# Up products of paired 256-token tiles as seven fp32 block products in the shared expert

## The chip, the cores and the metric

The kernel runs on one NeuronCore of a Trainium2 chip. The engines are TensorE (PE, matrix products into PSUM), VectorE (DVE), ScalarE (ACT), GpSimd (POOL) and SyncE (SP, which here only issues DMA). Each engine works through its own instruction list in order and waits on semaphores that other engines or DMA transfers raise. The metric is the device time of one execution in microseconds. Before the change it is 723.63 us (median of three runs, 723.37 to 724.58).

## What is computed

All data are fp32. Sixteen sequences of 128 tokens with 256 features pass through a cross-attention layer (16 heads of 64) with a residual, then through a mixture of experts with a residual:

```
x = x + attention(context, layernorm(x), cond)          # per sequence
h = layernorm(x)                                        # 2048 tokens x 256
scores = h @ router                                     # 2048 x 8
expert = argmax(scores); gate = sigmoid(max score)      # top 1
shared = (silu(h @ ws1) * (h @ ws3)) @ ws2              # ws1, ws3: 256 x 704; ws2: 704 x 256
routed = silu(gate*h @ w1[e]) * (gate*h @ w3[e]) @ w2[e]
out = x + shared + routed
```

The change concerns `shared` alone, and the order in which parts of it run.

## The kernel before

**Stages.** The attention runs over pairs of sequences (`g` = 0 to 7) in steps `u` of eight heads. In most steps (`seven_step`) the key and value projections are made as seven block products instead of eight; `plain_step` is used for `u` = 0, 1 and 31. `seven_step` is built of `product` (TensorE), `hold` (a ScalarE copy out of PSUM) and `join` (a VectorE add). A step makes logits on TensorE, negated row maxima on VectorE (L672), exponentials on ScalarE (L679), a division by the row sums on GpSimd (L692), a transposition in 32x32 blocks on VectorE (L701) and through DRAM (L705, L713), and then the weighted sums on TensorE (L725) for the step before.

After that, normalised tokens are transposed into `hT` (feature by token), the router's scores decide the expert of each token (`route`, a chain of many small VectorE operations), and eight expert windows are worked through: `up` (L1607 to L1620), `out_rows` (L1640), which adds the residual and the shared part gathered from `s_rows`, and an indirect scatter to `out` (L1645).

**The shared expert.** Its tokens form eight tiles of `TB` = 256. Of the 704 hidden columns, `FC` = 5 blocks of 128 are full; the last 64 columns of `ws1` and of `ws3` share one block. For a tile, `hidden(t, mid, f)` makes for a full block two products with 256-long sums, that is four fp32 products of 128 x 128 by 128 x 256 (L164), silu on ScalarE (L179) and a multiply on VectorE (L180); the narrow block takes two products. `down` makes 12 products (L194), adds the residual (L201) and stores to `s_rows`. A tile so has 22 + 12 products.

The generator `shared_expert` yields after each block, and `shared_unit()` advances it by one piece wherever TensorE would have to wait: in the last two attention steps, between the last projections, and in the routing chain (one piece for each step of `route`). The down products of a tile are made after the hidden blocks of the next one. Tile 7 is kept to the end (`held`): its hidden block 0 before the last window's down products, the rest after them. It reads `out` back (L236), after every scatter, adds its rows (L254) and stores them (L255).

**Order and memory.** The order on each engine is written out by hand: instructions run in the order in which the Python code calls them. PSUM has three pools: `ps_s` (two tiles of two banks), `ps_m` (three of one bank, tag `mm`, shared by `hidden`, `down` and most other users) and `ps_o` (one). A tile's wait is derived from who last read or wrote it.

Of the kernel before, what the change touches and what calls it, by code (L numbers as in the profile page):

```python
# [9 lines left out]
F32 = mybir.dt.float32  # L10
I32 = mybir.dt.int32
AF = mybir.ActivationFunctionType
ALU = mybir.AluOpType
# [4 lines left out]
P = 128  # L18
# [9 lines left out]
def resampler_attn__then__top1_moe_kernel(  # L28
# [160 lines left out]
    def down(t, mid, xr):  # L189
        rows = slice(t * TB, (t + 1) * TB)  # L190
        py = ps_m.tile([P, 2, D], F32, tag="mm", name=f"ys_{t}")
        for i in range(2):
            for f in range(FC + 1):
                nc.tensor.matmul(  # L194
                    py[:, i, :],
                    lhsT=mid[:, f, ts(i, P)],
                    rhs=shared["wd"][:, f, :],
                    start=(f == 0),
                    stop=(f == FC),
                )  # L200
        nc.vector.tensor_tensor(xr, py, xr, ALU.add)  # L201
        nc.gpsimd.dma_start(out=s_rows[rows, :].rearrange("(b p) d -> p b d", p=P), in_=xr)

    def shared_expert():


        pend = None
        for t in range(NT // TB - 1):
            rows = slice(t * TB, (t + 1) * TB)
            xr = mwork.tile([P, 2, D], F32, tag="xr", name=f"xr_{t}", bufs=3)  # L210
            nc.gpsimd.dma_start(out=xr, in_=x_rows[rows, :].rearrange("(b p) d -> p b d", p=P))
            mid = mwork.tile([P, FC + 1, TB], F32, tag="mid", name=f"mid_{t}")
            nc.gpsimd.memset(mid[0 : P - FR, FC, :], 0.0)
            for f in range(FC + 1):
                hidden(t, mid, f)
                yield
            if pend is not None:
                down(*pend)
                yield
            pend = (t, mid, xr)  # L220
        yield "last"
        down(*pend)
        yield
# [3 lines left out]
    def held(mid):  # L227

        t = NT // TB - 1
        xr = mwork.tile([P, 2, D], F32, tag="xr", name=f"xr_{t}", bufs=3)  # L230
        nc.gpsimd.memset(mid[0 : P - FR, FC, :], 0.0)
        for f in range(FC + 1):
            hidden(t, mid, f)
            yield
        for i in range(2):
            load = nc.sync.dma_start(out=xr[:, i, :], in_=out[B - 2 + i])  # L236
            for s in scattered:
                tc.add_manual_dep(
                    load.ins,
                    s.ins.name,  # L240
                    mybir.DependencyInfo(mybir.DependencyClass.Sync, mybir.DependencyReason.DATA),
                    reason="rows of any token may come from any tile",
                )
        for i in range(2):
            py = ps_m.tile([P, D], F32, tag="mm", name=f"ys_{t}_{i}")
            for f in range(FC + 1):
                nc.tensor.matmul(
                    py,
                    lhsT=mid[:, f, ts(i, P)],
                    rhs=shared["wd"][:, f, :],  # L250
                    start=(f == 0),
                    stop=(f == FC),
                )
            nc.vector.tensor_tensor(xr[:, i, :], py, xr[:, i, :], ALU.add)  # L254
            nc.sync.dma_start(out=out[B - 2 + i], in_=xr[:, i, :])  # L255

    def shared_unit():
        return next(stream, None)


    with ExitStack() as at:
# [565 lines left out]
        def norms(gt, gh):  # L827
# [27 lines left out]
            def h_stats():  # L855
                rows = slice(2 * gh * S, (2 * gh + 2) * S)
                xr = xres[gh]
                nc.sync.dma_start(
                    out=x_rows[rows, :].rearrange("(b p) d -> p b d", p=P), in_=xr
                )  # L860
                mv = st["hmv"] = small.tile([P, 2, 2], F32, tag="hmv", name=f"hmv_{gh}")
                for i in range(2):
                    s6 = small.tile([P, 6], F32, tag="hst", name=f"hst_{gh}_{i}")
                    nc.vector.bn_stats(s6, xr[:, i, :])
                    nc.vector.bn_aggr(mv[:, i, :], s6)
# [105 lines left out]
        def plain_step(u, units, side=(), behind=()):  # L971
# [15 lines left out]
            nm = maxima(u, 1, ps[1])  # L987
            unit()
            normalise(u, 0)
            exponents(u, 1, ps[1], nm)  # L990
# [111 lines left out]
        for g in range(NG):  # L1102
# [89 lines left out]
            else:  # L1192
                seven_step(
                    u + 2, Seven("v", g, 1), (), {}, (h_on("h_stats", "h_variances"), roots, (), ()),
# [6 lines left out]
        keep_heads(2 * B - 2)  # L1201
        finish(B - 2)
        for j in range(3):
            shared_unit()
# [3 lines left out]
        shared_unit()  # L1208
# [9 lines left out]
        shared_unit()  # L1218
# [7 lines left out]
    mscratch = scratch.enter_context(tc.tile_pool(name="mscratch", bufs=1))  # L1226

# [4 lines left out]
    w2s = [wexp.tile([P, NF, D], F32, name=f"w2_{k}") for k in range(5)]  # L1232

# [77 lines left out]
    def route():  # L1311
# [57 lines left out]
        pc = ps_m.tile([P, 2, B * E], F32, tag="mm", name="counts")  # L1369
# [172 lines left out]
    def transpose_pair(pair):  # L1542

        px = ps_m.tile([P, DC, 2, P], F32, tag="mm", name=f"px_{pair[0]}")
# [4 lines left out]
        if pair[0] == 0:  # L1549
            nc.vector.tensor_copy(  # L1550
                inputs_t[0][:, :, 0 : 2 * P], px.rearrange("p c i q -> p c (i q)")
# [131 lines left out]
    for w in range(E):  # L1683
        for f in range(NF):
            up(w13s[w % 3], inputs_t[w % NREST], WINDOWS[w], mids[w % 5], f, f"w{w}")
            if f == 0:
# [10 lines left out]
                else:  # L1697
                    shared_unit()
# [9 lines left out]
    def ending():  # L1708
        rest = held(mids[E % 5][:, :, 0:TB])
# [137 lines left out]
```

## Time and profile before

| | us |
|---|---|
| median of three runs | 723.63 |
| profiled execution | 724.18 |
| its span | 722.5 |
| TensorE busy | 708.2 |
| VectorE busy | 415.3 |
| ScalarE busy | 295.0 |
| GpSimd busy | 287.5 |

The span is the profiled execution from its first to its last instruction. Mean granted TensorE clock is 0.995 of full speed. In the timeline, the shared expert begins at 440.24 us; the last attention product of line 725 begins at 473.26, the first expert window at 569.56, and the last down products of tile 7 at 713.02. How a profile row reads: the line of the kernel, engine, operation, the tile written and those read, shape and count; then busy time, mean duration of one in nanoseconds, and the engine's idle time just before, with what ended most of it. In a timeline row come the start, the length, and in brackets the idle time before it. In a row of stretches come, for each engine, busy time and number of instructions, then the granted clock, the DMA share and GB/s.

### The profile page before, as it was taken

The numbers are of one execution on the slowest core, as the hardware profiler recorded it, in microseconds if no ns is written. First come the engines' busy times: TensorE is split into PE (matmuls) and PEld (weight loads), VectorE is DVE, ScalarE is ACT, GpSimd is POOL, SyncE is SP. The second block draws the span as 40 slices with busy tenths as digits, with TensorE's granted clock in tenths as the row PEclk, the third lists the DMA queues.
The fourth block names the chain that finished last, engine by engine and source line by source line (L and its number), as shares of the span: only waits on it lengthen the run. The fifth ranks groups of instructions, "written<-read, shape, count | busy, mean of one in ns | idle before, by whom it ended". The sixth has DMA issues, their size and how long they took to land.

```text
span 722.5 us, 11941 instructions
## 1 busy us (share of the span) xinstructions
PE 708.2 (98%) x4228; PEld 594.8 (82%) x4228; DVE 415.3 (57%) x941; ACT 295.0 (41%) x855; POOL 287.5 (40%) x449
## 2 busy tenths in 40 slices
PE   9999999999999999999999999899899999999997
PEld 6778888888888888888888887688798878878886
DVE  6568678777777777777766766325623333323321
ACT  3555475475475366466466456412111111101111
POOL 4358346346346345435433622311032234434220
PEclk9999999999999999999999999999999999999999
DMA  8266755864864865765764765341393136666601
GB/s 277 73 218 198 219 172 183 242 191 163 252 191 158 253 193 168 235 196 181 206 194 156 255 186 179 104 116 34 129 364 107 44 88 167 198 195 181 188 29 46
DMA packets 140470, 125.20 MB, mean 173 GB/s; under 512 B 61615, under 2 KB 124594, under 8 KB 140404
## 3 DMA queue, kind: packets, MB, share of 16 engines
q1 hardware_dynamic: 135892, 111.46, 49.8%
q0 software_dynamic: 4224, 12.65, 5.5%
q8 instruction: 35, 0.57, 0.3%
q14 instruction: 31, 0.25, 0.1%
q10 hardware_dynamic: 288, 0.26, 0.1%
HBM read 75.59 MB, written 48.92 MB: 172 GB/s over the span
## 4 chain that ended last, share of the span: by engine, by line
PE 92%; DVE 3%; ACT 3%; DMA 2%; issue 1%; ACTq 0%
PE u_w L1607 10%; PE O L725 8%; PE p L164 8%; PE pw L744 8%; PE S L660 8%; PE pq L487 8%; PE yr L1640 6%; PE ys L194 5%; PE skX L606 5%; PE svX L606 5%; PE svZ L606 3%; PE svY L606 3%; PE skZ L606 3%; PE skY L606 3%; ACT pe L679 1%; PE ur_w L1607 1%
## 5 line engine op out<-in xcount | busy, mean ns | idle before, releaser
L692 POOL TENSOR_SCALAR pe<-pe,rs 128x256 f32<-128x256 f32 x256 | 130.4, 526 | 227.3 <-DVE rs L689 227.3
L679 ACT ACTIVATE pe<-S,nmx 128x256 f32<-128x256 f32 x256 | 119.0, 483 | 54.8 <-DVE nmx L672 54.8
L672 DVE TENSOR_REDUCE nmx<-S 128x4 f32<-128x1024 f32 x64 | 75.4, 1219 | 30.9 <-PE S L660 30.9
L701 DVE STREAM_TRANSPOSE px<-pe 128x512 f32<-128x512 f32 x128 | 82.2, 682 | 0.1
L164 PE MATMUL p<-hT,ws 128*128 128x256 f32 x320 | 73.9, 387 | 3.4 <-DVE mid L180 3.3
L1607 PE MATMUL u_w<-xT,w 128*128 128x256 f32 (+2 forms) x320 | 77.1, 396 | 0.0
L164 PEld LDWEIGHTS p<-hT,ws 128*128 128x128 f32 x320 | 61.3, 194 | 13.1 <-DVE mid L180 3.7
L1607 PEld LDWEIGHTS u_w<-xT,w 128*128 128x128 f32 x320 | 60.7, 190 | 13.7 <-issue 0.4
L744 PE MATMUL pw<-wo,oT 128*128 128x256 f32 x256 | 66.3, 385 | 0.0
L487 PE MATMUL pq<-kvT,early 128*128 128x256 f32 x256 | 65.8, 385 | 0.0
L725 PEld LDWEIGHTS O<-pT,v 128*64 128x64 f32 x1024 | 55.2, 137 | 12.3 <-issue 5.6
L725 PE MATMUL O<-pT,v 128*64 128x128 f32 x1024 | 63.2, 276 | 1.4 <-DMA pT<-p_blocks 1.4
L660 PE MATMUL S<-kT,qT 64*128 64x256 f32 x512 | 63.9, 389 | 0.0
L1615 ACT ACTIVATE rsl_w<-u_w 128x256 f32<-128x256 f32 (+2 forms) x40 | 16.0, 400 | 110.6 <-PE u_w L1607 89.2
L487 PEld LDWEIGHTS pq<-kvT,early 128*128 128x128 f32 x256 | 47.5, 190 | 11.0 <-issue 5.1
L736 ACT COPY oT<-O 128x512 f32<-128x512 f32 x32 | 18.7, 586 | 92.2 <-PE O L725 92.2
L744 PEld LDWEIGHTS pw<-wo,oT 128*128 128x128 f32 x256 | 47.4, 190 | 10.6 <-issue 4.8
L660 PEld LDWEIGHTS S<-kT,qT 64*128 64x128 f32 x512 | 46.8, 186 | 10.5 <-issue 6.2
L179 ACT ACTIVATE sl<-p 128x256 f32<-128x256 f32 x40 | 15.2, 383 | 96.9 <-PE p L164 96.9
L679 ACT ACTIVATION_READ_ACCUMULATOR pe<-S,nmx 128x1 f32 x256 | 54.5, 213 | 0.0
L1616 DVE TENSOR_TENSOR mid_w<-u_w,rsl_w 128x256 f32<-128x256 f32 (+2 forms) x40 | 17.8, 445 | 60.3 <-ACT rsl_w L1615 56.1
L1640 PE MATMUL yr<-w,mid_w 128*128 128x256 f32 (+1 forms) x252 | 48.0, 379 | 0.0
(269 smaller groups left out, 1151.1 us busy)
## 6 DMA issues: line engine op xcount, KB each, us to landing
p_blocks<-px SPq DMA_DIRECT2D x64, 512.0 KB
pT<-p_blocks SPq DMA_DIRECT2D x64, 512.0 KB
w<-in_w_dram SPq DMA_DIRECT2D x16, 640.0 KB
w<-in_w_dram SPq DMA_DIRECT2D x8, 704.0 KB
t_blocks<-tx SPq DMA_DIRECT2D x12, 256.0 KB
kvT<-t_blocks SPq DMA_DIRECT2D x12, 256.0 KB
h_rows<-h SPq DMA_DIRECT2D x8, 256.0 KB
xres<-in_x_dram SPq DMA_DIRECT2D x7, 256.0 KB
```

Of the source, the lines that this page charges most:

```text
L164: nc.tensor.matmul(ps, lhsT=shared["w13"][:, c, ds(col, P)], rhs=hT[:, c, ts(t, TB)], start=(c == 0), stop=(c == DC - 1),)
L487: nc.tensor.matmul(pqs[g, j][:, jj], lhsT=wq[:, c, ts(2 * j + jj, P)], rhs=kvTs[g][:, c, :, 1, :], start=(c == 0), stop=(c == DC - 1),)
L606: nc.tensor.matmul(o[:, a, :], lhsT=left, rhs=right, start=(first and a == 0), stop=(a == 1), skip_group_check=True,)
L660: nc.tensor.matmul(pl[:, r, j, :], lhsT=qTs[g, h][rows, k, i, :], rhs=kTs[g, h][rows, i, k, :], start=True, stop=True,)
L672: nc.vector.tensor_reduce(nmx, pl, AX.X, ALU.max, negate=True)
L679: nc.scalar.activation(pes[u][:, h, :], pl[:, r, j, :], AF.Exp, bias=nmx[:, r, j : j + 1], accum_out=sums[u][:, h : h + 1],)
L692: nc.gpsimd.tensor_scalar(w, w, rs[:, i : i + 1], 1.0, ALU.mult, ALU.mult)
L701: nc.vector.transpose(px[:, :, t].rearrange("p j h q -> p h j q"), pes[u][:, ts(n, 4), ts(t, S)].rearrange("p h (j k) -> p h j k", k=BL),)
L725: nc.tensor.matmul(o[r * HD : (r + 1) * HD, j, :], lhsT=vs[g, h][:, i, t, ts(2 * j + r, HD)], rhs=pTs[u][:, j // 2, :, t, 2 * (j % 2) + r, :],
L744: nc.tensor.matmul(pws[b], lhsT=outT[u][:, k % HC, :], rhs=wo[:, k, :], start=(k == 0), stop=(k == NP - 1))
L1607: nc.tensor.matmul(ps[:, k, 0:n], lhsT=w13[:, c, ds(col, P)], rhs=xT[:, c, 0:n], start=(c == 0), stop=(c == DC - 1),)
L1640: nc.tensor.matmul(py[rows, :], lhsT=mid[:, f, :], rhs=wd[:, f, :], start=(f == 0), stop=(f == NF - 1))
```

## The change

1. **Tiles 0 and 1** are made as before. Their down products are now given out in two halves.
2. **Tiles 2 to 7** are taken in three pairs (`pair`, k = 1, 3, 2 in this order). The two sums over 256 features for two matrices (`ws1`, `ws3`) and two tiles are a 2 x 2 by 2 x 2 block product. It is made with seven products a block instead of eight, from sums and differences of weight blocks (`pair_weights`) and of token blocks (`pair_tokens`), both on GpSimd. `place` gives the order of the products in TensorE's list. The partial results meet in PSUM: two X tiles used in turn for even and odd blocks, and one tile whose halves are Y and Z. These three take all of `ps_m` while the pairs run. Three results of a block are copied out by ScalarE, and four adds or multiplies on VectorE and one multiply on GpSimd make the hidden values. The narrow block keeps two products a tile (`left`).
3. **Pair 3** (tiles 6 and 7, the last 512 tokens) writes its hidden values into a buffer `held`; its four half down products and their adds to `out` come at the end, the first before the last window's down products, the second right after them. The loads and stores of `out` alternate between SyncE's and ScalarE's queues.
4. **In `plain_step`** for `u` > 1, the second four heads' exponentials are issued before the shared-expert piece instead of after it. In the last `seven_step`, the Newton steps of the layer norm move behind the join of Y and the hold of X (from the second to the third group of `sides`).
5. The number of pieces given out between the last attention projections changes, `x` of the pair g = 6 goes to `s_rows` instead of `x_rows` (its shared part is added at the end), and three other users of `ps_m` (`counts`, the transposes of gathered rows, the down products) use `ps_s`.

The products by number, and where each is placed (7f + offset):

```
n  offset  writes  operands (weights x tokens)        after it
1    0     X       w1[0]      x a0                     ACT copies X to hs0
5    2     Z       s1         x tt0                    ACT copies Z to high
2    3     Y       w1[1]      x a1                     DVE hs0 = Y + hs0; ACT silu
6    4     X +=    s2         x tt1                    ACT copies X to hs1
3    6     Z +=    s4         x b1                     DVE hs1 = Z + hs1; ACT silu
7    8     X +=    (w1[0]-w3[0]) x tt2                 DVE high = X + high; POOL high *= hs1
4   12     X +=    w3[1]      x tt3                    DVE low = X * hs0
```

The core of the diff:

```diff
+    def pair_tokens(k):
+        ...
+        op = nc.gpsimd.tensor_tensor
+        op(tt[:, 0], blk(0, 1), blk(0, 0), ALU.subtract)
+        op(tt[:, 1], blk(1, 1), tt[:, 0], ALU.subtract)
+        op(tt[:, 2], blk(1, 1), blk(0, 1), ALU.subtract)
+        op(tt[:, 3], blk(1, 0), tt[:, 1], ALU.subtract)
+    def pair_weights(f):
+        ...
+        op(s1, up_block(1, 0, f), up_block(1, 1, f), ALU.add)
+        op(s2, s1, up_block(0, 0, f), ALU.subtract)
+        op(up_block(1, 0, f), up_block(0, 0, f), up_block(1, 0, f), ALU.subtract)
+        op(s4, up_block(0, 1, f), s2, ALU.subtract)
+        def step(n, f):
+            X = shared["X"][f % 2]
+            Y, Z = shared["YZ"]
+            low, high = (m[:, f, :] for m in mids)
+            if n == 1:
+                hs[f] = shared["pool"].tile([P, 2, TB], F32, tag="hs", name=f"hs_{k}_{f}", bufs=3)
+                multiply(1, f, X, True)
+                nc.scalar.copy(hs[f][:, 0], X)
+                if f:
+                    nc.scalar.activation(hs[f - 1][:, 1], hs[f - 1][:, 1], AF.Silu)
+            elif n == 5:
+                multiply(5, f, Z, True)
+                nc.scalar.copy(high, Z)
+            elif n == 2:
+                multiply(2, f, Y, False)
+                nc.vector.tensor_tensor(hs[f][:, 0], Y, hs[f][:, 0], ALU.add)
+            ...
+        for f in range(FC):
+            for at, n in ((0, 1), (2, 5), (3, 2), (4, 6), (6, 3), (8, 7), (12, 4)):
+                place[7 * f + at] = lambda n=n, f=f: step(n, f)
+        for n, at in enumerate((0, 2, 3, 4)):
+            place[7 * FC + at] = lambda n=n: left(n // DC, n % DC)
     def shared_expert():
-        for t in range(NT // TB - 1):
+        for t in range(2):
+        ...
+        shared["X"] = [ps_m.tile([P, TB], F32, tag="mm", name=f"pX_{k}") for k in range(2)]
+        yz = ps_m.tile([P, 2, TB], F32, tag="mm", name="pYZ")
+        shared["YZ"] = [yz[:, k, :] for k in range(2)]
+        pair_tokens(1)
+        for f in range(FC):
+            pair_weights(f)
+            if f == 0:
+                pair_tokens(3)
+        yield from down(*pend.pop(0), ps_s, "S")
+        for k in (1, 3, 2):
+        ...
+    def held():
+        ...
+        half(0)
         yield
+        half(1)
+        for n in range(4):
+            load = ways[n % 2].dma_start(out=xrs[n // 2][:, n % 2, :], in_=out[B - 4 + n])
+        ...
+        for n in range(4):
+            if n > 1:
+                half(n)
+            xr = xrs[n // 2][:, n % 2, :]
+            nc.vector.tensor_tensor(xr, pys[n], xr, ALU.add)
+            ways[n % 2].dma_start(out=out[B - 4 + n], in_=xr)
@@ plain_step
             nm = maxima(u, 1, ps[1])
+            if u > 1:
+                exponents(u, 1, ps[1], nm)
             unit()
             normalise(u, 0)
-            exponents(u, 1, ps[1], nm)
+            if u < 2:
+                exponents(u, 1, ps[1], nm)
@@ last seven_step
-                    u + 2, Seven("v", g, 1), (), {}, (h_on("h_stats", "h_variances"), roots, (), ()),
+                    u + 2, Seven("v", g, 1), (), {}, (h_on("h_stats", "h_variances"), (), roots, ()),
```

## The prediction

> **What bounds the kernel now.** First the engine totals, the clock row and the chain of the page.
>
> ```profile
> PE 708.2 (98%) x4228; PEld 594.8 (82%) x4228; DVE 415.3 (57%) x941; ACT 295.0 (41%) x855; POOL 287.5 (40%) x449
> ...
> PEclk9999999999999999999999999999999999999999
> ...
> PE 92%; DVE 3%; ACT 3%; DMA 2%; issue 1%; ACTq 0%
> ```
>
> TensorE is busy for 98% of the span and carries 92% of the chain, so a removed product should shorten the kernel, and an added gap on TensorE should lengthen it by its own length. Next, the timeline of TensorE where the shared expert runs (start, length, what, and in brackets the idle time before it).
>
> ```profile
> 453.00 1.03 PE L164 MATMUL pr<-hT,ws 128*128 128x256 f32 x4
> 457.37 5.24 PE L164 MATMUL p<-hT,ws 128*128 128x256 f32 x16 [3.34 <-DVE mid L180]
> ...
> 484.76 7.07 PE L164 MATMUL p<-hT,ws 128*128 128x256 f32 x32
> ...
> 513.79 7.13 PE L194 MATMUL ys<-wsd,mid 128*128 128x256 f32 x24 [2.03 <-DVE mid L180]
> ```
>
> Each fp32 product is two records. The 32 records take 6.91 us on the chain (484.92 to 491.83): 0.432 us a product. The row at 457.37 needs 5.24 us for 16 records that take 3.6 elsewhere; the one at 513.79 needs 7.13 for 24 that take 5.34. One-microsecond windows say why (third number from the right: granted clock).
>
> ```profile
> 456.00:457.00 1.00, 0.00 (x0) 0.00 (x0) 0.11 (x1) 0.99 (x3) 0.00 (x0) 1.00 0.00 0
> ...
> 458.00:459.00 1.00, 1.00 (x4) 0.82 (x3) 0.24 (x1) 0.00 (x0) 1.00 (x4) 0.50 0.00 0
> ...
> 516.00:517.00 1.00, 1.00 (x3) 0.73 (x3) 0.87 (x4) 0.00 (x0) 0.00 (x0) 0.50 0.00 0
> ```
>
> After each of these two gaps the clock is halved for some 3.4 us, which costs another 1.7 and 1.8 us. Last, the price of a hand-over between engines.
>
> ```profile
> 432.57 0.58 ACT L625 COPY v<-svX 128x512 f32<-128x512 f32 x1
> ...
> 433.20 1.13 PE L606 MATMUL svX<-v_sums,kvT 128*128 128x256 f32 x4
> 434.17 1.03 PE L606 MATMUL svY<-wv,kvT 128*128 128x256 f32 x4
> ...
> 437.35 1.13 PE L606 MATMUL svY<-wv,kvT 128*128 128x256 f32 x4 [1.13 <-DVE v L630]
> ...
> 692.50 0.38 ACT L1615 ACTIVATE rsl_w<-u_w 128x256 f32<-128x256 f32 x1 [6.52 <-PE u_w L1607]
> 692.91 0.42 DVE L1616 TENSOR_TENSOR mid_w<-u_w,rsl_w 128x256 f32<-128x256 f32 x1 [1.72 <-ACT rsl_w L1615]
> ```
>
> The product train at 690.57 has issued eight records by 692.30; ScalarE starts at 692.50: 0.20 us from the end of a product's slot to the reader's start. A 128x256 read takes 0.38 us on ScalarE and 0.42 on VectorE. TensorE goes on 0.05 us after the reader ends (433.15 to 433.20), and a product group so restarted takes 0.97 us instead of 0.86: 0.11 lost.
>
> **The products removed.** Per tile pair and 128-column block f, eight products become seven: 3 pairs x 5 blocks = 15 products x 0.432 = **-6.5 us**. The down products only change place.
>
> **The gap at 513.79.** It stands where the ScalarE table for the sigmoid and the routing work of VectorE hold up tile 3's hidden products. That code is gone; its successor is costed under pair 1. Removed: 2.03 + 1.8 = **-3.8 us**.
>
> **Exponentials and Newton steps in front.** ScalarE now runs, from 450.24, table load (1.28), silu, table load (1.28), four exponentials (1.9), table load (1.28), silu. With all eight exponentials first, one load remains. The Newton operations (434.2 to 436.7) no longer stand ahead of the join L630, so the product at 437.35 starts at 435.96; of the 1.4 us won, 0.75 goes back, as the second shared-expert product now waits for the bank that L632 frees. Stepping on at full clock, the hidden multiply of block 2 ends near 453.2, `pr_0` waits 1.2 us instead of the next group waiting 3.34, and the fourth block of tile 1 ends near 457.7, not 462.5. The last softmax half comes back transposed about 465.4 (5.9 us from transposes to landing before), 0.6 us too late for its product. Net **-4.4 us**.
> [...] A gap of 1.13 us (437.35) left the clock at 1.00, so I leave 1.2 us unthrottled.
>
> **The new waits on TensorE.** The order of a block in the built program is P1(f), P7(f-1), P5(f), P2(f), P6(f), P4(f-1), P3(f). Y and Z are halves of one PSUM tile, and the program's waits treat them as one: P2, which writes Y, waits for ScalarE's copy of Z (L272), which waits for P5, the product right in front of it. From P5's slot end: 0.20 + 0.38 + 0.05 = 0.63, + 0.11 restart = **0.75 us** in each block. Queued behind P2 are P6, P4 and P3, hence everything. Then P1(f+2) waits for the multiply that reads P4(f) (L291), with only P3 between: 0.20 + 0.42 + 0.05 - 0.43 = 0.24, + 0.11 = **0.35**. In block 0, without P4, P3 waits as long for the add of P2 (L275).
> A block then takes 4.1 us instead of 3.0. ScalarE's five reads (1.9 us) and VectorE's four (1.7) fit, so neither is the bound; the round trip is.
> - Pair 2: 5 x 0.75 + 0.35 + 3 x 0.35; then in the narrow products the third waits for silu and multiply of the first half, 0.20 + 0.38 + 0.03 + 0.43 + 0.05 + 0.11 = 1.2. Sum 6.4.
> - Pair 3: the eight gather transposes stand between one P5 and P2, so 4 x 0.75; 0.35 + 2 x 0.35; 0.7 because four gate multiplies (0.34 each) and six copies stand on VectorE before the adds; 1.2 as above; 1.2 because pair 2's P1 waits for L291 behind the last narrow multiply. Sum 7.1.
> - Pair 1 shares VectorE with the routing chain, whose operations (9 in 2.1 us, 18 in 3.5 us, then 5 + 5, two of 1.2 us) now stand ahead of adds that TensorE waits for. Stepped through: 5 x 0.75, and 0.85, 1.25, 1.75, 1.25, 1.1 at P3(0), P5(1), P3(1), P1(3), P1(4). Sum 9.95. These reach about 2.3 us of idle in 3.4, so I add half of one throttling, 0.85.
>
> Together **+24.3 us**. [...] A block idles 1.1 us in 4.1, and at most some 1.4 in 3.4 us; 1.13 left the clock whole, 2.03 did not. [...]
>
> **GpSimd.** 28 token and weight sums are new: eight 128x256 at 0.73 us (row below), twenty 128x128 at an estimated 0.46 (between 0.73 and the 0.22 of 128x16). They start near 2.1 us after the router's last product; the first weight sum is ready at 5.5, and P5(0) asks at 6.1: hidden, and each later one is earlier than VectorE lets its product be. With that cover gone, the whole would cost up to 10 us in pair 1. Behind them wait the store of tile 1's rows, two residual loads and memsets; their readers are 10 us away. Pair 2's token sums (2.9 us) run under pair 3's tail.
>
> ```profile
> L563 POOL TENSOR_TENSOR kvT<-kvT 128x256 f32<-128x256 f32 x8 | 5.8, 729 | 0.6
> ```
>
> **The tail.**
>
> ```profile
> 706.82 0.99 POOL L1645 DMA_INDIRECT out_dram<-sg,table  x1 [2.22 <-DMA out_dram<-sg,table]
> ...
> 709.15 1.01 SPq L236 DMA_DIRECT2D xr<-out_dram  x2
> ```
>
> The loads of `out` wait for the last scatter and start 3.9 us after the last routed product; they now have 18 products (7.8 us) behind that product to hide under instead of 30 (13 us). No row shows their landing; the scatter took 2.3 us from issue to its waiter, so I take 2.3 (bounds 2 and 4). The fourth half product needs the bank of the first, which is free after its add at 6.7 us; TensorE would come at 5.2. **+1.7 us** (1.3 to 3.4). Two loads go to ScalarE's queue, where only stores stand behind them.
> The writes of tile 6's rows, the moved PSUM pools and the yields cost nothing: the same transfers and instructions, with no wait that ends late.
>
> **Sum.** On the profiled span 722.5: -6.5 - 3.8 - 4.4 + 24.3 + 1.7 = 733.8. The runs' median 723.63 lies 1.1 above that span (the profiled run itself took 724.18): **735 us**.
>
> **Rivals.**
> - *The hand-overs keep pace.* The attention's own seven-product step runs with a few tenths of idle, and if the P2 wait were hidden, each pair would run at TensorE's pace. For: the engines have room. Against: the program's wait on the directly preceding product. Only pair 1's routing (5 us) and the tail stay: 722.5 - 14.7 + 5 + 1.7 = 714.5, 716 as a run. It decides for faster when all pair stalls together stay under 13.0 us, 0.87 a block; I have 1.6.
> [...]
> - *Milder stalls*: routing overlaps the P2 waits and restarts cost nothing: 14 x 0.75 falls to 14 x 0.63, pair 1 loses 6 us: 727.
>
> **How the numbers follow.** The step-by-step case has 0.68 (731 to 739), the gate 0.12, the milder case 0.10, faster 0.08, no change 0.02; 0.2% is about what the runs can tell from no change. Slower 0.90. 727 to 742 leaves out the faster cases, half of the milder and the worst of the gate.
>
> **What would show it.** L256 products: 210 records; idle of TensorE before P2 with ScalarE's L272 as releaser, 0.6 to 0.8 us some 14 times: if it is under 0.3, the main step is wrong. Before P1 with L291: 0.2 to 0.4. No gap near 3.3 us, and the clock at 1.00 in the plain step. In pair 1 gaps over 1 us ended by L275, L282 or L291. Idle of TensorE grows from 14 to about 33 us. The last half product waits for the first add by 1 to 2 us. [...]

## The result

The changed kernel takes 752.7 us (median of four runs, 747.0 to 754.32), the kernel before 723.5 in the same comparison. The ratio of the means, with a fifth run of 751.2, is 1.0387, 95% interval 1.0339 to 1.0434. The forecast was slower, 735 us, with a range up to 742: the sign was right, the size fell short by 17.7 us. The profiled execution was the quickest of the changed kernel's: 747.0 us with a span of 745.1 and a mean TensorE clock of 0.994; the others show spans of 749.5 to 752.4 and clocks of 0.980 to 0.988. So 22.6 us can be read in the trace (745.1 against 722.5); some 6 more (747.0 to the median) are not in it, and the lower clocks of the other runs say that they are mostly clock.

First the engine totals and the clock row of the page of the changed kernel.

```profile
PE 709.0 (95%) x4198; PEld 585.7 (79%) x4198; DVE 435.1 (58%) x972; ACT 307.6 (41%) x898; POOL 314.0 (42%) x494
...
PEclk9999999999999999999999999998999999999999
```

TensorE is as long busy as before with 30 records fewer (part of them at half clock), and its idle time has grown from 14 us to 36. The timeline of TensorE says where. The front (the stretch up to the router's last product) in the kernel before, in three rows:

```profile
440.24 3.72 PE L164 MATMUL p<-hT,ws 128*128 128x256 f32 x16
...
467.99 5.34 PE L164 MATMUL p<-hT,ws 128*128 128x256 f32 x24
473.26 1.97 PE L725 MATMUL O<-pT,v 128*64 128x128 f32 x32
```

In the changed kernel:

```profile
437.67 1.06 PE L952 MATMUL pr<-wr,hT 128*128 128x8 f32 x8 [0.28 <-ACT v L771]
...
441.49 3.72 PE L164 MATMUL p<-hT,ws 128*128 128x256 f32 x16 [1.79 <-DVE v L778]
...
455.50 1.13 PE L164 MATMUL pr<-hT,ws 128*128 128x256 f32 x4 [1.09 <-DVE mid L180]
456.47 3.62 PE L164 MATMUL p<-hT,ws 128*128 128x256 f32 x16
...
467.88 1.09 PE L871 MATMUL O<-pT,v 128*64 128x128 f32 x16 [0.52 <-DMA pT<-p_blocks]
471.21 1.09 PE L871 MATMUL O<-pT,v 128*64 128x128 f32 x16 [2.23 <-DMA pT<-p_blocks]
```

The gap of 3.34 us ahead of the group of 16 is gone, as forecast, and `pr` waits 1.09 (forecast 1.2). New are 1.79 us for the bank that the join (L778) frees, and 2.75 us (0.52 and 2.23) for the transposed softmax block ahead of the last attention product. In the kernel before, 24 records of the shared expert stand right ahead of that product and it does not wait. The router's last product ends at 487.75 instead of 495.53; 20 products (8.63 us) of the shared expert have moved behind it, so 0.85 us are lost, of which 0.28 are there already at 430: the front has lost 0.6 us where 4.4 were to be won.

In the pairs, rows of pair 1 (493.69 to 530.2) and the start of pair 2 (565.06):

```profile
495.18 0.70 PE L256 MATMUL pYZ<-hT,ws 128*128 128x256 f32 x2 [0.46 <-ACT mid L272]
...
497.69 0.67 PE L256 MATMUL pYZ<-hT,shared_sums 128*128 128x256 f32 x2 [1.37 <-DVE hs L275]
...
501.13 0.67 PE L256 MATMUL pYZ<-tt,shared_sums 128*128 128x256 f32 x2 [1.91 <-POOL ws L237]
...
507.91 1.19 PE L256 MATMUL pYZ<-hT,shared_sums 128*128 128x256 f32 x2 [4.08 <-POOL mid L359]
508.89 1.06 PE L256 MATMUL pX<-hT,ws 128*128 128x256 f32 x2
...
562.55 1.13 PE L299 MATMUL pr<-hT,ws 128*128 128x256 f32 x4 [0.93 <-DVE held L309]
...
565.06 0.70 PE L256 MATMUL pX<-hT,ws 128*128 128x256 f32 x2 [0.95 <-DVE held L291]
565.60 0.59 PE L256 MATMUL pYZ<-tt,shared_sums 128*128 128x256 f32 x2
566.66 0.70 PE L256 MATMUL pYZ<-hT,ws 128*128 128x256 f32 x2 [0.46 <-ACT mid L272]
```

P5 to P2 takes 1.06 us (565.60 to 566.66) instead of 0.43, 14 times, with L272 as the releaser: the wait of P2 as forecast. The two large gaps of pair 1 name GpSimd, which had long been done; VectorE's adds ended just before (L282 at 500.99, L275 at 507.76). After the gap of 4.08 a row of two records takes 1.06 instead of 0.59: half clock (0.50 in the stretches from 507 to 513). Over pair 1 the mean clock is 0.91, over pairs 2 and 3 it is 1.00. The end waits as forecast, 2.01 for the first bank:

```profile
737.39 2.86 PE L191 MATMUL yh<-wsd,held 128*128 128x256 f32 x12 [2.01 <-DVE xrh L400]
```

### The profile page after: what moved, and what is told of

Same layout as the page of the kernel before. It is cut to its first block, busy times and chain, and to the rows that moved or that the text cites. A ratio compares the mean times of both kernels' runs of the same rounds, so it can differ in the third digit from the quotient of the medians.

```text
span 745.1 us, 12032 instructions
## 1 busy us (share of the span) xinstructions
PE 709.0 (95%) x4198; PEld 585.7 (79%) x4198; DVE 435.1 (58%) x972; ACT 307.6 (41%) x898; POOL 314.0 (42%) x494
## 5 line engine op out<-in xcount | busy, mean ns | idle before, releaser
L1763 DVE TENSOR_TENSOR mid_w<-u_w,rsl_w 128x256 f32<-128x256 f32 (+2 forms) x40 | 17.8, 446 | 60.4 <-ACT rsl_w L1762 58.4
L1787 PEld LDWEIGHTS yr<-w,mid_w 128*128 128x128 f32 (+1 forms) x252 | 39.3, 171 | 7.5 <-issue 0.3
L835 DVE RECIPROCAL rs<-sums 128x4 f32<-128x4 f32 x64 | 11.3, 176 | 52.7 <-ACT pe L825 52.5
L1792 POOL DMA_INDIRECT out_dram<-sg,table x18 | 18.1, 1004 | 50.5 <-DVE sg L1790 23.1
```

Source lines behind the costliest of these rows:

```text
L1787: nc.tensor.matmul(py[rows, :], lhsT=mid[:, f, :], rhs=wd[:, f, :], start=(f == 0), stop=(f == NF - 1))
L1792: nc.gpsimd.indirect_dma_start(out=out.rearrange("b s d -> (b s) d"), out_offset=Offset(ap=routing["table"][0:n, t : t + 1], axis=0), in_= ...
```

## The experiments

Each time is the median of 4 to 10 runs, and the brackets hold its ratio to the kernel before with a 95% interval; the kernel before had medians of 722.6 to 723.5 beside them. "Less" is against the median of the changed kernel, whose own runs spread over 7.3 us, so such a difference is good to a few us.

### The waits of the pairs

Y in a bank of its own. In this run Y keeps adding up from block to block, so its hidden values are not the reference's; TensorE's instructions are the same.

```diff
-        yz = ps_m.tile([P, 2, TB], F32, tag="mm", name="pYZ")
-        shared["YZ"] = [yz[:, k, :] for k in range(2)]
+        yz = [ps_o.tile([P, TB], F32, tag="O", name="pY"), ps_m.tile([P, TB], F32, tag="mm", name="pZ")]
+        shared["YZ"] = yz
```

> The changed kernel with Y in a PSUM bank of its own (the one that the last attention product and the slot table used; the slot table goes to the pool of the wide tiles). Theory 1, the wait of P2 on ScalarE's copy of Z is the main loss: 14 waits of 0.72 us go, of the span of the profiled execution 745 some 10 us go, pair 2 takes 19.3 us instead of 23.3, pair 3 about 20 instead of 23.4; the typical run goes from 752 to 741. Theory 2, VectorE is what limits the pairs: the wait moves to P1, P3 and P5 (L291, L275, L282) and less than 4 us are won, 748. Theory 3, the idle of P2 also costs granted clock in the typical runs: their mean clock returns from 0.98-0.99 to 0.995 or more, the spread between runs (747 to 754) shrinks below 2 us, and the median falls by 14 or more, to 738.

Measured: 739.0 (ratio 1.0239, 1.0192 to 1.0285), 13.7 less. Pair 2 takes 19.2 us (560.88 to 580.08), as theory 1 had it, pair 3 with its boundary 22.0 instead of 24.5, but pair 1 34.8 instead of 36.5: its gaps only move, one of 4.26 and one of 3.52 us. So P2's wait is real and removable in pairs 2 and 3, and in pair 1 VectorE sets the pace. The span is 8.5 less than in the profiled execution of the changed kernel; the other 5 of the medians' difference would be clock that this execution had not lost, which no trace here shows. The clocks of the four runs, 0.985 to 0.993, and their spread of 5.7 us speak against theory 3: the P2 idles are not what throttles.

Then all waits that the order of products makes, on top of Y's own bank:

```diff
-            for at, n in ((0, 1), (2, 5), (3, 2), (4, 6), (6, 3), (8, 7), (12, 4)):
+            for at, n in ((0, 1), (2, 5), (3, 2), (5, 6), (6, 3), (8, 7), (11, 4)):
...
-        for n, at in enumerate((0, 2, 3, 4)):
+        for n, at in enumerate((-4.5, -3.5, 2, 3)):
...
-            X = shared["X"][f % 2]
+            X = shared["X"][(f + k) % 2]
...
-                multiply(2, f, Y, False)
+                multiply(2, f, Y, True)
```

> The changed kernel with all waits of the pairs that the order of its products makes taken out at once: Y in a bank of its own, P4 of the block before ahead of P6, the first tile's two narrow products inside the last block, and the two X banks exchanged from pair to pair. Theory 1, the rest of the pairs' loss is the listed waits: pair 2 takes 16.9 us (39 products of 0.432; 23.3 in the changed kernel, 19.2 with Y alone), pair 3 17.7 instead of 24.5, pair 1 still some 34, as VectorE's chain sets it; span 730, median about 731.5. Theory 2, ScalarE or VectorE is too slow for TensorE's pace once the waits are gone: pair 2 stays above 18.5 us, 735 or more.

Measured: 734.86 (1.0157, 1.0140 to 1.0174). Pair 2 takes 17.7 us (560.46 to 578.20), pair 3 19.3, pair 1 34.2. Above the 16.9 of theory 1 stand one wait for a token sum and a few short waits and restarts. The start of pair 2:

```profile
561.40 0.70 PE L256 MATMUL pZ<-tt,shared_sums 128*128 128x256 f32 x2 [0.34 <-POOL tt L223]
561.93 0.59 PE L256 MATMUL pY<-hT,ws 128*128 128x256 f32 x2
562.37 0.59 PE L256 MATMUL pX<-tt,shared_sums 128*128 128x256 f32 x2
562.80 0.59 PE L256 MATMUL pZ<-hT,shared_sums 128*128 128x256 f32 x2
563.23 0.59 PE L256 MATMUL pX<-hT,ws 128*128 128x256 f32 x2
```

Products follow each other at 0.43: ScalarE and VectorE keep pace where nothing else uses them. In pair 2 theory 2 falls (17.7 is under its 18.5); pair 1 is slow as both theories have it, and the median lies 3.4 above that of theory 1.

### GpSimd's sums beside the routing chain

All sums left out, plain blocks in their place, so this run does not make the shared expert's values:

```diff
-        pair_tokens(1)
-        for f in range(FC):
-            pair_weights(f)
-            if f == 0:
-                pair_tokens(3)
...
-                5: (sums[:, 0, ts(f, P)], tt[:, 0]),
+                5: (up_block(1, 0, f), cols[0][1]),
```

> The changed kernel with all 32 token and weight sums on GpSimd left out; the seven products take plain blocks of the weights and tokens instead, so the shared expert's output for six tiles is not the reference's. TensorE's instructions are the same. Theory 1, VectorE's routing operations are slowed by GpSimd's sums running beside them: run copies back from 0.58 to 0.18 us, the hit operations from 0.70 to 0.29, shift from 0.38 to 0.17; pair 1 takes 29 us instead of 36.5 and the half clock in it is gone; median 752 to 744 or less. Theory 2, the operations are slow for another reason, or the products wait for the sums themselves: in the first case their durations stay and the time changes by less than 1 us; in the second the durations stay and the gap at P5(0) goes, 2 us.

Measured: 742.7 (1.0273, 1.0235 to 1.0311), 10.0 less. Pair 1 takes 29.6 us (497.32 to 526.89) with the clock whole (1.00, against 0.91), pairs 2 and 3 what they took. VectorE's groups in the routing chain between 487 and 515 us (count, busy us and mean ns, idle before); `hit`, `run`, `shift`, `tile_f` and `first` are small tiles of that chain. First the kernel before:

```profile
L1354 DVE TENSOR_TENSOR hit<-hit,rank 128x128 f32<-128x128 f32 x1 | 0.3, 292 | 0.0
L1359 DVE TENSOR_REDUCE first<-hit 128x16 f32<-128x128 f32 x1 | 0.3, 285 | 0.0
...
L1242 DVE COPY run<-run 128x64 f32<-128x64 f32 x1 | 0.2, 195 | 0.0
L1255 DVE CAST tile_f<-tile_i 128x16 f32<-128x16 int32 x1 | 0.2, 176 | 0.0
L1431 DVE SCALAR_TENSOR_TENSOR shift<-win,shift 128x16 f32<-128x16 f32 x1 | 0.2, 175 | 0.0
```

The changed kernel:

```profile
L275 DVE TENSOR_TENSOR hs<-pYZ,hs 128x256 f32<-128x256 f32 x3 | 1.3, 419 | 2.1 <-PE pYZ L256 2.1
L1402 DVE CAST tile_f<-tile_i 128x16 f32<-128x16 int32 x1 | 1.2, 1231 | 0.0
...
L1501 DVE TENSOR_TENSOR hit<-hit,rank 128x128 f32<-128x128 f32 x1 | 0.7, 703 | 0.0
...
L1389 DVE COPY run<-run 128x64 f32<-128x64 f32 x1 | 0.6, 599 | 0.0
...
L1578 DVE SCALAR_TENSOR_TENSOR shift<-win,shift 128x16 f32<-128x16 f32 x1 | 0.4, 378 | 0.0
...
L1506 DVE TENSOR_REDUCE first<-hit 128x16 f32<-128x128 f32 x1 | 0.3, 286 | 0.0
```

Without the sums:

```profile
L1492 DVE TENSOR_TENSOR hit<-hit,rank 128x128 f32<-128x128 f32 x1 | 0.3, 293 | 0.0
...
L1569 DVE SCALAR_TENSOR_TENSOR shift<-win,shift 128x16 f32<-128x16 f32 x1 | 0.2, 174 | 0.0
L1393 DVE CAST tile_f<-tile_i 128x16 f32<-128x16 int32 x1 | 0.2, 174 | 0.0
```

The same operation takes 0.29, 0.70 and 0.29 us; a shift 0.18, 0.38 and 0.17. A reduction (0.285, 0.286) and the adds that read PSUM (0.42) take the same in all: what is slowed here has its operands in SBUF and is no reduction. The cast of 1.23 us ran while GpSimd issued three DMAs (505.03 to 507.21). Three groups of the chain (count to run, key to win, slot to row) took 1.9, 2.1 and 3.5 us before and 3.3, 3.2 and 6.2 after; 1.05 of these 5.2 us are the cast. Not every such operation is slowed: the adds right behind the run copies took 0.24 in the mean as before (0.25). Without the sums the same three DMA issues come earlier, beside the run copies, and the last of these takes 0.48; the operations shown are back at their old times. Theory 1 holds, with GpSimd's DMA issues as a second, smaller part.

Two more runs, on a kernel with four things mended (below): the sums left out again,

> The run before with all 32 token and weight sums left out (plain blocks in their place, so six tiles of the shared expert are not the reference's). Theory 1, what is left in pair 1 is GpSimd's sums holding VectorE's routing operations: 7 us less than the run with four things mended, and the clock whole in pair 1. Theory 2, the routing chain itself, on VectorE ahead of the pair's additions, is the larger part: under 3 us less.

measured 722.08 (0.9981, 0.9965 to 0.9997) against 727.13 with them: 5.05 less, pair 1 28.7 us instead of 33.6. That is between the two theories (7, and under 3), and pair 1 keeps a gap of 2.37 us with half clock behind it: the chain itself costs TensorE time too. And four of the sums moved out of the chain:

```diff
-            if f == 0:
-                pair_tokens(3)
...
+            if k == 1:
+                pair_tokens(3)
```

> The run with four things mended, with the token sums of the second pair (four of 128x256, 2.9 us of GpSimd) taken from the middle of the routing chain to the end of pair 1. Theory 1, each us of GpSimd beside the chain costs VectorE about a half (5.2 us in 15): 1.4 us less. Theory 2, P5 of the second block waits for sums that now come earlier, and VectorE's chain is as late as before: no change within 0.5.

measured 726.04, 1.1 less, with intervals that overlap (1.0028 to 1.0053 against 1.0037 to 1.0083): the direction of theory 1, not more.

### The front

Each of the two edits there alone, on the kernel before. The exponentials:

```diff
+            if u > 1:
+                exponents(u, 1, ps[1], nm)
             unit()
             normalise(u, 0)
-            exponents(u, 1, ps[1], nm)
+            if u < 2:
+                exponents(u, 1, ps[1], nm)
```

> The kernel before with only the exponentials of the last two softmax halves moved ahead. Theory 1, the reading of the prediction (gap of 3.34 us and the half clock after it go, 1.2 us come): 719.5, 4 below the kernel before. Theory 2, the transposed softmax block comes too late for its product and eats what is won in the plain step: O_31 waits 2 to 3 us, 722.5.

Measured 718.92 (0.9947, 0.9933 to 0.9961): 4.0 less, theory 1; the last attention product does not wait there. The Newton steps:

```diff
-(h_on("h_stats", "h_variances"), roots, (), ()),
+(h_on("h_stats", "h_variances"), (), roots, ()),
```

> The kernel before with only the inverse roots' Newton operations moved from the second place of the last seven-product step to the third. The prediction had a gain of 0.65: 722.9. The trace of the changed kernel says a loss: a shared expert product waits 1.8 us for the bank freed by the join, and one more 0.3: 724.5, a loss of about 1.0.

Measured 728.11 (1.0059, 1.0040 to 1.0078): 5.15 more, far beyond both numbers. TensorE's timeline of this run, then its one-microsecond stretches (the third number from the right is the granted clock):

```profile
441.29 6.76 PE L164 MATMUL p<-hT,ws 128*128 128x256 f32 x16 [1.82 <-DVE v L632]
447.98 1.97 PE L725 MATMUL O<-pT,v 128*64 128x128 f32 x32
449.88 2.00 PE L660 MATMUL S<-kT,qT 64*128 64x256 f32 x16
```

```profile
439.00:440.00 1.00, 0.47 (x3) 0.07 (x1) 1.00 (x3) 0.00 (x0) 1.00 (x3) 1.00 0.00 0
440.00:441.00 1.00, 0.00 (x0) 0.00 (x0) 0.90 (x2) 0.00 (x0) 1.00 (x2) 0.83 0.55 225
441.00:442.00 1.00, 0.71 (x2) 0.62 (x3) 1.00 (x4) 0.00 (x0) 0.83 (x2) 0.50 0.74 299
...
446.00:447.00 1.00, 1.00 (x4) 0.72 (x3) 0.00 (x0) 0.00 (x0) 0.00 (x0) 0.50 1.05 374
```

The wait for the join's bank costs 1.0 us net, and the clock is halved for nearly the whole group behind it: 6.76 us instead of 3.72, another 3.0. The product S starts at 449.88 instead of 445.79. Five of the seven runs took 728 with a clock of 0.991, two 726 with 0.995: how much clock is lost differs from run to run. In the profiled execution of the changed kernel the same gap of 1.79 us cost no clock (the group takes 3.72). Undone in the changed kernel:

> The changed kernel with the Newton operations back in the second place of the last seven-product step. Theory 1, their move costs the same here as alone (5.2 us: a wait of 1.8 us for the bank freed by the join, and the half clock that follows it in most runs): 752.7 to 747.5, and the spread of the runs shrinks. Theory 2, the clock that is lost after this gap would be lost later in any case (at the gap of some 2 us before the last attention product): only the gap itself is won, 1.0 us, 751.7.

Measured 746.2 (1.0312, 1.0290 to 1.0335): 6.5 less, theory 1.

The exponentials undone in the changed kernel:

> The changed kernel with the exponentials back in their old place. Theory 1, they are worth here what they are worth alone, 4 us: 752.7 to 756.7. Theory 2, most of it is given back in the changed kernel, as the last attention product waits for its transposed softmax block, and a block that comes later under a front that is as much later waits no longer: less than 2 us, 754.

Measured 750.79 (1.0399, 1.0350 to 1.0449): 1.9 less, where both theories had more. Its interval and the changed kernel's (1.0339 to 1.0434) nearly coincide, so the times do not settle what the exponentials are worth there. The traces say more. With the exponentials back, TensorE waits 3.35 and 2.07 us in the front, 5.42 in all; in the changed kernel the same places show 1.09, 0.52 and 2.23, 3.84 in all. So of the 4 us some 1.6 are left, as theory 2 has it. And here the long gap costs no clock, since the group behind it takes 3.72:

```profile
460.63 3.72 PE L164 MATMUL p<-hT,ws 128*128 128x256 f32 x16 [3.35 <-DVE mid L180]
```

Two units (pieces of the shared expert) put back ahead of the last attention product:

```diff
         finish(B - 2)
+        shared_unit()
+        shared_unit()
         weigh(2 * B - 1)
...
-            if i % 2 == 1:
+            if i % 4 == 3:
                 shared_unit()
```

> The changed kernel with two of the shared expert's units (tile 1's fifth block and its narrow product) moved from the preparation of the last two images' router input to a place ahead of the last attention product, where the kernel before has them. Theory 1, the front has too few products for both places, since tile 2's have gone into the pairs: the waits for the transposed softmax block (2.2 and 0.5 us) go, and waits of the same size come before the router's last products: 752.7, within 1.5. Theory 2, the second place has slack: 2.5 us faster, 750.

Measured 744.77 (1.0308, 1.0272 to 1.0345): 7.9 less, more than theory 2 had. The product no longer waits:

```profile
468.21 3.62 PE L164 MATMUL p<-hT,ws 128*128 128x256 f32 x16
471.76 1.97 PE L871 MATMUL O<-pT,v 128*64 128x128 f32 x32
473.66 1.13 PE L164 MATMUL pr<-hT,ws 128*128 128x256 f32 x4
```

and nothing waits in its stead before the router's products. Of the 7.9, 2.75 are wait, and more is clock behind it: in the run without sums, which has this wait too (0.42 and 2.01), the three groups behind it take 1.98, 3.78 and 4.04 us instead of 1.09, 1.99 and 3.62, 3.1 us lost. Where the other 2 us of the medians' difference lie is not shown.

### The end

The fourth half product in a bank of its own:

```diff
+            if n < 3:
                 py = ps_m.tile([P, D], F32, tag="mm", name=f"yh_{n}")
+            else:
+                py = ps_s.tile([P, 2, 2 * D], F32, tag="S", name=f"yh_{n}")[:, 0, 0:D]
```

> The changed kernel with the fourth half product at the end in a PSUM bank of its own. The span after the last scatter's issue is 13.45 us in the changed kernel (731.65 to 745.1). Theory 1, the bank alone makes the end late: 2.0 us less, 752.7 to 750.7. Theory 2, the loads of the last rows land late as well and set the last additions: the additions then wait for them and 1.2 to 1.5 us are won, 751.3.

Measured 749.67 (1.0378, 1.0333 to 1.0424); the intervals overlap, so the trace decides: from the last scatter's issue to the end 11.8 us instead of 13.45, and the four additions run in one go from 742.92, when the loads of `out` have landed. Theory 2: 1.65 us.

### Do they add up?

> The changed kernel with four things mended together: pair waits out, Newton steps in their old place, two units ahead of the last attention product, fourth half product in its own bank. Theory 1, the single gains (17.8, 6.5, 7.9 and 3.0 us) share the clock that is lost behind the gaps: from the trace, TensorE's work of 701.7, pair 1's stalls of some 15, the front's 1.1, pairs 2 and 3 some 2, the end's 4.5: 724, median 725. Theory 2, they add up: 752.7 - 35.2 = 717.5.

Pair waits, Newton steps, the two units and the end mended at once: 727.13 (1.0060, 1.0037 to 1.0083). Theory 1. The single gains add up to 35 us, the four together bring 25.6. That they overlap in the clock that gaps cost, as theory 1 has it, fits these times but is not shown in a trace.

### Do seven products pay?

Down products in the pool of the wide tiles, on the kernel before with the exponentials in front:

```diff
-        py = ps_m.tile([P, 2, D], F32, tag="mm", name=f"ys_{t}")
+        py = ps_s.tile([P, 2, 2 * D], F32, tag="S", name=f"ys_{t}")[:, :, 0:D]
```

> The kernel before with the exponentials in front, and the accumulators of the shared expert's down products in the pool of the wide PSUM tiles instead of the pool of the up products. Theory 1, the gap of 2.0 us behind tile 3's narrow product is a wait for a bank that VectorE's late multiply frees, and the down products, which need no other bank, run in it: 718.9 to 716.9, without a gap over 1 us between 500 and 540. Theory 2, the next tile's products then wait for the same multiplies: the gap moves behind the down products, 718.5 or more.

Measured 716.26 (0.9904, 0.9888 to 0.9921), with no gap over 1 us between 500 and 540: theory 1. Then tiles 0 to 3 plain, pairs only for the last four tiles:

```diff
-        for t in range(2):
+        for t in range(4):
...
-        for k in (1, 3, 2):
+        for k in (3, 2):
```

> Tiles 0 to 3 with eight products beside the routing as in the kernel before, two pairs (tiles 6 and 7, then 4 and 5) with seven products in the order of the run with all pair waits out, exponentials in front, Newton steps in their old place, down products in the wide pool, the fourth half product at the end in a bank of its own. Theory 1, products saved are worth their time once nothing waits: 10 x 0.432 = 4.3 us below the run with the exponentials and the wide pool (716.9), less up to 2 us of sums that start only after tile 3: 713 to 715. Theory 2, the sums on GpSimd and the rest of the routing chain hold each other up: the first pair waits 5 us or more, 718 or more.

Measured 722.15 (0.9982, 0.9972 to 0.9992): theory 2 in kind, for another reason than it names. Pair 2 runs at pace (17.75 us), but in pair 3 a copy of ScalarE waits 4.98 us for a buffer that a gate multiply (`high *= hs1`) on GpSimd must free, and this stands behind four gathers, which stand behind the sums; TensorE waits 3.49 us for it. The gate multiplies on VectorE:

```diff
-                nc.gpsimd.tensor_tensor(high, high, hs[f][:, 1], ALU.mult)
+                nc.vector.tensor_tensor(high, high, hs[f][:, 1], ALU.mult)
```

> The run with two pairs, with the gate multiplies of the pairs on VectorE instead of GpSimd, where four gathers stood ahead of them. Theory 1, the wait of 3.5 us in the first pair and the half clock after it (1.9 us) go: 722.15 to 716.8. Theory 2, VectorE then holds up TensorE instead, with five reads a block in 3.0 us beside the gates and copies of the gathered rows: 719 or more.

Measured 722.78 (1.0002, 0.9983 to 1.0021), the number of theory 2. That wait goes, and the transposes of the gathered rows wait instead:

```profile
537.72 0.41 PE L1701 MATMUL px<-ident,xg 128*128 128x128 f32 x2 [0.57 <-DVE xg L1686]
539.00 0.44 PE L1701 MATMUL px<-ident,xg 128*128 128x128 f32 x2 [0.88 <-DVE xg L1686]
543.36 1.11 PE L1701 MATMUL px<-ident,xg 128*128 128x128 f32 x4 [3.93 <-DVE xT L1703]
```

Last, the sums of two blocks behind the gathers:

```diff
-        for f in range(FC):
+        for f in range(3):
             pair_weights(f)
...
-            yield from pair(k, mids)
+            for n, _ in enumerate(pair(k, mids)):
+                if k == 3 and n in (3, 4):
+                    pair_weights(n)
+                yield
```

> The run with two pairs and gate multiplies on VectorE, with the weight sums of the last two blocks behind the first four gathers on GpSimd. Theory 1, the transposes of the gathered rows waited for gathers that stood behind all sums (waits of 0.6, 0.9 and 3.9 us and half a clock's loss): they go, 722.8 to 716.5. Theory 2, they wait for VectorE, whose gate multiplies and copies stand behind the pair's additions: 720 or more.

Measured 716.06 (0.9899, 0.9877 to 0.9922), theory 1; one transpose still waits:

```profile
531.56 0.70 PE L256 MATMUL pZ<-tt,shared_sums 128*128 128x256 f32 x2 [0.64 <-POOL shared_sums L235]
...
538.46 0.66 PE L1704 MATMUL px<-ident,xg 128*128 128x128 f32 x4 [1.40 <-DVE xT L1706]
```

So the gathers that stood behind the sums were the larger part. This kernel (716.06) and the plain one with the exponentials in front and the down products in the wide pool (716.26) are both 1.0% faster than the kernel before and cannot be told apart. Ten products fewer (4.3 us) are worth nothing yet: the two waits shown take 2.0 us, and from the last product to the last store it takes some 1.4 us longer (5.5 against 4.1), with 512 instead of 256 held tokens. The rest is not accounted for.

## Why the prediction was right in sign and far short in size

Three terms failed. The front, put at -4.4 us, came to +0.6. GpSimd's sums, put at nothing ("P5(0) asks at 6.1: hidden"), slowed VectorE's routing chain, and pair 1, put at +10.8, came to +16.3. The way from the profiled span to the median, put at 1.1, came to 7.6, as the other executions lose clock that the profiled one did not (0.980 to 0.988 against 0.994). These are 5.0, 5.5 and 6.5 of the 17.7 us. Term by term, predicted and then read in the profiled execution:

| term of the sum | predicted | measured |
|---|---|---|
| 15 products fewer | -6.5 | -6.5 (0.43 a product) |
| gap at 513.79 and its clock | -3.8 | -3.8 (gone) |
| front | -4.4 | +0.6 |
| pair 2 | +6.4 | +6.4 |
| pair 3 and its boundary | +7.1 | +6.8 |
| pair 1 | +10.8 | +16.3 |
| wait at the end, last store | +1.7 | +2.8 |
| span | 733.8 | 745.1 |
| median over span | 1.1 | 7.6 |

**What held.** The wait of P2, from the program's waits and three durations, came within 0.03 us of its 0.75 (0.62 beyond the slot of P5 and 0.10 of restart), and with it pairs 2 and 3; that Y and Z in one tile cause it is shown by the run that parts them. The exponentials alone bring 4.0 on the kernel before, as expected of that run from their part of the sum. The rival in which hand-overs keep pace was wrong for this order of products and right for another (0.43 a product once the waits are out).

**The front** failed in two steps. "of the 1.4 us won, 0.75 goes back": the Newton steps now stand ahead of L778, whose bank the next shared product needs, for a gap of 1.79 us and not 0.75. The prediction left the clock whole because "1.13 us (437.35) left the clock at 1.00", but the move makes a longer gap than that: alone it costs 5.15 us, 3.0 of them clock. And "0.6 us too late for its product" was 2.75. The second half of the transposed block was there 9.6 us after the last transposition (461.63 to 471.21), not 5.9. In all seven profiled runs that wait for it, it is 9.0 to 9.6. In the kernel before nothing waits for it: the last transposition ends at 464.15, and the second half of its product begins some 10 us later, so no wait there shows the 5.9, and two more shared units stood in the time. The prediction named the changed number of units, "the yields cost nothing"; that was the wrong line to pass over. Putting two back won 7.9. These two steps make 1.6 and 2.15 of the 5.0 us; the rest of the front is not traced to one step.

**Pair 1** failed at "P5(0) asks at 6.1: hidden". The sums were indeed never late in pair 1. They cost because VectorE's routing operations, ahead of the adds that TensorE waits for, ran beside them and beside the DMA issues that follow: 5.2 us more on the three groups. The run without sums gives back 6.9 us in pair 1, its half clock with it, and 4.9 of 5.05 us on top of the mended kernel. In most rows two-input operations and copies in SBUF are up by 0.1 to 0.4 us each (a hit operation from 0.29 to 0.70, a run copy from 0.20 to 0.60), the reduction is unchanged at 0.286, and so are the adds that read PSUM, at 0.42. Some two-input operations stay at their old time (the adds behind the run copies, 0.24 against 0.25); what sets these apart is not shown. I weighed the sums only as work that must be ready in time, not by what they do to the engine beside them.

**The clock.** The 0.12 for "the gate" stood for a clock halved again and again in the pairs, at some 10 us. No run shows this term: the P2 idles of 0.6 us did not throttle (pairs 2 and 3 show 1.00). Nor does one show that waits add up over 3.4 us, as the 0.85 in pair 1 counts them (half of one throttling): in the profiled execution the half clock there stands behind the single gap of 4.08 us (0.50 from 507 to 513, 0.91 over the pair). Longer gaps than the P2 idles did throttle, those from 1.13 to 3.35 us not in every execution. The "1.13 us (437.35)" with the clock at 1.00 was one execution: behind the same gap the clock is 0.50 from 439 to 442 in the run with the Newton steps undone, and four records there (L752) take 1.95 us instead of 1.11; three more profiled runs show 0.50 behind it. The prediction took half clock after the 2.03 us at 513.79 from one execution; in the run with the exponentials alone the same gap costs nothing, 5.45 us for the group instead of 7.13:

```profile
509.76 5.45 PE L194 MATMUL ys<-wsd,mid 128*128 128x256 f32 x24 [2.02 <-DVE mid L180]
```

So a gap has no fixed price in clock, and part of the -3.8 is what that execution happened to lose. Of the 7.6 us of the median over the span, 1.9 lie around the span in the profiled run too; 5.7 are left. The run with the fourth half product in its own bank has the same order of work up to the end, and its profiled execution shows where such time can go: it ends the router's last product 5.3 us later than the changed kernel's. Of these, 2.2 are there already at 430 (an attention product starts at 429.75 instead of 427.54; the mean clock of the whole run is 0.988 against 0.994), where nothing was changed, and 3.1 come with the half clock behind the gaps of 1.80 and 2.09 us. Pair 1 takes 36.5 us there too.

**The end** was right in kind (a wait of 2.0, and 0.1 of restart, for 1.7); the loads landed 2.7 us after their issue (3.4 and 3.6 in the runs where they set the end), not 2.3, and from the last addition to the end it takes 0.7 longer.

What stays open: how the 5.7 us divide in the other executions of the changed kernel, and what decides whether a gap costs clock.

## What to carry to other kernels

Work given to an idle engine is not free just because it is ready in time: look whether the engine beside it carries a chain that something waits for. Here operations of that chain with their operands in SBUF went from 0.29 to 0.70 us, and pair 1 took 6.9 us more than without the sums. When filler work is taken out of one stage to be done better in another, recount what the first stage still has to put ahead of each of its waits. Do not let a product be followed at once by one that writes the other half of the same PSUM tile: the second waits for the reader of the first, 0.73 us each time here.

## What the runs showed that was not expected

- The same gap of 1.8 us ahead of the same group cost from nothing (3.72 us for the group) to 3.0 us (6.76), with 5.41, 5.33 and 5.25 in other runs; a gap of 3.35 us once cost nothing.
- A cast of 128x16 took 1.23 us instead of 0.18 beside three DMA issues of GpSimd, and a shift of integers 1.44 instead of 0.17 beside the same issues in the run with Y in its own bank.
- Four repairs that alone brought 17.8, 7.9, 6.5 and 3.0 us brought 25.6 together: savings from single gaps are not a sum.
